# Four graph layers on one core: the 26 source tiles grouped as 4, 6, 6, 6, 4 instead of 6, 6, 6, 4, 4

## The chip, the cores and the metric

The kernel runs on one core of one Trainium2 chip. A core has five engines that work side by side, each through its own queue of instructions in order: TensorE (PE; its weight loads are listed apart as PEld), VectorE (DVE), ScalarE (ACT), GpSimd (POOL) and SyncE (SP), which here only issues transfers. They meet through semaphores. The metric is the device time of one execution in microseconds (us).

## What is computed

Four layers over a graph of 3327 nodes with 512 features and a dense 0/1 adjacency matrix. The first three are attention layers with 8, 4 and 8 heads, the last averages over neighbours. Each is applied to a normalised copy and added to the input:

```python
x = x + L0(relu(layernorm(x)), adj)     # 8 heads of 64
x = x + L1(relu(layernorm(x)), adj)     # 4 heads of 128, self loops added
x = x + L2(relu(layernorm(x)), adj)     # 8 heads of 64
x = x + L3(relu(layernorm(x)), adj)     # mean over neighbours, two dense layers

# an attention layer, for each head
e = leaky_relu(s1[:, None] + s2[None, :], 0.2)      # s1 = Wh @ a1, s2 = Wh @ a2
p = softmax(where(adj > 0, e, -inf), axis=1)
out = elu(p @ Wh)

# the last layer
agg = (adj > 0) @ x / max(degree, 1)
out = relu(concat(x @ W_self + b_self, agg @ W_nb + b_nb) @ W_comb + b_comb)
```

All of it is float32 in the reference.

## The kernel before

Layers are numbered `l` = 0 to 3 in the code; "the second layer" is `l == 1`.

**The two sides of leaky_relu.** exp(leaky_relu(s1 + s2)) is one product of a row factor and a column factor where s1 + s2 > 0, and another one where it is not. So a head needs two 0/1 matrices instead of real weights: the edges with a positive sum ("side" 0) and the edges with a negative sum (side 1). The column factors are multiplied into the projected features beforehand, the row factors after the sum.

**Tiles and groups.** The nodes are 26 tiles of 128. Target tiles are taken in seven chunks of four (the last has two). Source tiles `j` are taken in five groups, `JG` (L67): 6, 6, 6, 4 and 4 tiles. `JM` is the largest group and sizes the buffers. `jwhere` tells a tile's group and its place there. A group is the unit of a mask tile (`m`), of a load of features (`ab`), of the 0/1 tile (`tht`, `gt`), and of the copy to float32r.

**One head of one chunk** (`attention`, L603). SyncE loads the row scores `s1b` (L624) and the features `ab` (L634 in the second layer, one load per side and group; L601 in the others). For each source tile, ScalarE (L656) or VectorE (L653; the tiles of `GP_ON_DVE`, in the second layer 18 to 25) writes whether s1 + s2 > 0. VectorE ANDs a group with its mask (L662): side 0. An XOR with the mask gives side 1: L666 into `gt` in layers 1 and 3, and L722 in place in the second layer, after all reads of side 0. Then TensorE multiplies. A pass (L672) runs two target tiles over all 26 source tiles, with the 0/1 tile as weights and the features as moving data; sums stay in PSUM. VectorE adds the pieces up (L708 or L712), and L730 to L737 scale the head's result.

**Precision by group in the second layer** (`KIND`, L49, one letter a group). A "b" group keeps the features as three bf16 pieces side by side, 387 columns (L690), and uses the fp8 0/1 tile directly. In an "s" or "v" group the features are split into two float32r pieces, 258 columns (L687). Then the 0/1 tile must be float32r too: `real` (L585, its copy is L590) makes it once for each pass and group, on ScalarE into `ts` (3 buffers) for "s", on VectorE into `tv` (2 buffers) for "v". `KIND` is "bssvv". In layers 1 and 3 all features are bf16 pieces, with two matmuls for each pair of tiles (L694, L697).

**Preparing the next layer.** While a layer runs, finished target tiles go through normalisation, projection (L388) and splitting (`pieces`, L341, with L359 to L369, or L423 and L426 for float32r groups) for the next one. `hooks.run` (L718) does a step of that after each pass. A scheduler then lays out each engine's queue.

**The output stage** (L885 on). The third layer's last tiles are projected (L443), VectorE adds the bias (L450) and SyncE stores the rows (L453). `load_y2` (L770) brings the last layer's features, one load per group, on GpSimd's queue: group 0 during the last head, the others after it. Masks are copied to float32r (`mf`, six buffers), odd groups on VectorE (L916), even ones on ScalarE (L918). TensorE multiplies (L921); chunk 0 takes its four targets together, group by group, the others one at a time. L930 and L931 finish a row.

**Buffers.** All memory of a layer is laid out by hand in `tags` (L849 to L852), with a count of buffers for each name. A buffer is written again when its last reader is done. In the second layer `ab` has seven and `tht` ten.

Of the kernel before, what the change touches and what calls it, by code (L numbers as in the profile page):

```python
# [29 lines left out]
FP8 = mybir.dt.float8e4  # L30
F32R = mybir.dt.float32r
# [6 lines left out]
P = 128  # L38
# [14 lines left out]
def tile_gnn(ctx: ExitStack, tc: tile.TileContext, x, adj, W0, a01, W1, al, ar, W2, a2,  # L53
# [7 lines left out]
    def pn(t):  # L61
        return min(P, N - t * P)

    PER = 4
    chunks = [(t, min(PER, NT - t)) for t in range(0, NT, PER)]
    where = {t0 + k: (c, k) for c, (t0, n) in enumerate(chunks) for k in range(n)}
    JG = [(0, 6), (6, 6), (12, 6), (18, 4), (22, 4)]  # L67
    JM = max(n for _, n in JG)
    jwhere = {j0 + i: (g, i) for g, (j0, n) in enumerate(JG) for i in range(n)}
    heads = [8, 4, 8]  # L70
# [28 lines left out]
                for l in range(1, 4)]  # L99
    maskd = [[dram.tile([P, nt, nj, P], FP8, name=f"mask_{c}_{g}") for g, (_, nj) in enumerate(JG)]  # L100
             for c, (_, nt) in enumerate(chunks)]
# [11 lines left out]
    for l in range(3):  # L113
        H, DA, AO, HW = dims(l)
        if l == 1:
            abd.append([dram.tile([H, 2, P, nj, AO], BF16, name=f"ab{l}_{g}") if KIND[g] == "b" else
                        dram.tile([H, 2, P, nj, 2 * DA], F32, name=f"ab{l}_{g}") for g, (_, nj) in enumerate(JG)])
        else:
            abd.append([dram.tile([H, P, nj, HW], BF16, name=f"ab{l}_{g}") for g, (_, nj) in enumerate(JG)])
    y1d = [dram.tile([n * P, D], F32, name=f"y1_{c}") for c, (_, n) in enumerate(chunks)]  # L120
    y2d = [dram.tile([P, nj, 2, D], F32, name=f"y2_{g}") for g, (_, nj) in enumerate(JG)]
    Xd = [dram.tile([D, D], F32, name=f"X{i}") for i in range(2)]
# [480 lines left out]
    def attention(L, hooks, open_next, close):  # L603

        l = L.l
# [3 lines left out]
        for c, (t0, nt) in enumerate(chunks):  # L609
            W = nt * P  # L610
            last = c + 1 == len(chunks)
            A = [mp.tile([P, D], F32, name="A", bufs=A_BUFS[l]) for _ in range(nt)]
            hook = 0
            for h in range(H):
# [10 lines left out]
                ab = []  # L625
# [17 lines left out]
                th, flip = [[], []], []  # L643
                for g, (j0, nj) in enumerate(JG):

                    pt = mp.tile([P, PER * JM * P], FP8, name="tht", bufs=10 if l == 1 else 7)
                    gt = pt if l == 1 else mp.tile([P, PER * JM * P], FP8, name="gt", bufs=7)
                    gv = gt[:, :nt * nj * P].rearrange("p (k j i) -> p k j i", k=nt, j=nj)
                    pv = pt[:, :nt * nj * P].rearrange("p (k j i) -> p k j i", k=nt, j=nj)
                    for jj in range(nj):  # L650
                        j = j0 + jj
                        if j in GP_ON_DVE[l]:
                            nc.vector.tensor_scalar(gv[:, :, jj, :], s1v, L.ns2[:, j, h:h + 1], 2.0,  # L653
                                                    op0=ALU.is_gt, op1=ALU.mult, saturate=False)
                        else:
                            nc.scalar.activation(gv[:, :, jj, :], s1v, AF.Relu, bias=L.ks2[:, j, h:h + 1], scale=BIG,  # L656
                                                 saturate=False)
                    flat = "p k j i -> p (k j i)"
                    mu = masks[g].rearrange(flat).bitcast(U32)
                    gu = gt[:, :nt * nj * P].bitcast(U32)  # L660
                    pu = pt[:, :nt * nj * P].bitcast(U32)
                    nc.vector.tensor_tensor(pu, gu, mu, ALU.bitwise_and)  # L662
                    if l == 1:
                        flip.append((pu, mu))
                    else:
                        nc.vector.tensor_tensor(gu, pu, mu, ALU.bitwise_xor)  # L666
                    th[0].append(pv)
                    th[1].append(gv)
                R = mp.tile([P, PER, 2, DA], F32, name="R", bufs=1)
# [150 lines left out]
    with tc.tile_pool(name="first", bufs=1) as fp:  # L820
# [21 lines left out]
        while hooks.tiles or hooks.flying:  # L842
# [5 lines left out]
    A, R = [("A", D, F32, n) for n in A_BUFS], ("R", PER * 2 * 129, F32, 1)  # L848
    ab, gt, tht = ("ab", JM * 400, BF16, 7), ("gt", PER * JM * P, FP8, 7), ("tht", PER * JM * P, FP8, 7)  # L849
    tags = [[A[0], R, tht, ("gap", 15 * 1024, FP8, 1), gt],  # L850
            [A[1], ("ab", JM * 258, F32R, 7), R, ("ts", 2 * JM * P, F32R, 3), ("tv", 2 * 4 * P, F32R, 2), tht[:3] + (10,)],
            [A[2], ab, ("R", PER * 2 * 65, F32, 1), tht, gt]]  # L852
    hooks.masks = [lambda t=t, g=g: load_mask(ip, t, g) for t in range(NT) for g in range(len(JG))][hooks.done:]
    for l in range(3):
        att = ExitStack()
        if l == 2:
            yp = main.enter_context(tc.tile_pool(name="early", bufs=1, side="right", reuse_waits="tile"))
        mp = att.enter_context(tc.tile_pool(name=f"att{l}", bufs=1, reuse_waits="tile"))
        lay_out(mp, *tags[l])
        nxt = []  # L860

        def open_next():
            nxt.extend([open_layer(l + 1), Fusion(l, load_comb(l)) if l < 2 else None])
            return nxt[0]

        def close():
            return nxt[1]
        attention(L, hooks, open_next, close)
        att.close()
        if l == 0:  # L870
            masking.close()
        L = nxt[0]
# [512 lines left out]
```

## Time and profile before

| what | us |
|---|---|
| median of 3 runs (lowest to highest) | 3606.12 (3604.16 to 3607.49) |
| the profiled execution: its time | 3609.94 |
| the profiled execution: its span | 3608.1 |
| first layer's preparation, before its first attention matmul | 0 to 185 |
| first attention layer | 185 to 1278 |
| second attention layer (first to last matmul of L690 and L687) | 1278 to 2120 |
| third attention layer, with the turn of layers | 2120 to 3253 |
| turn to the output stage, and the output stage | 3253 to 3608 |

The stretches are from the first and last starts of the matmul lines. Within the second layer the matmuls of L687 and L690 are busy for 334.2 (on `ts`), 220.0 (on `tv`) and 226.1 us, L590's copies for 300.3 us on ScalarE and 145.9 on VectorE.

How to read the profile: the page shows one execution. A group line gives line, engine, operation, tiles (written <- read), shapes and count, then busy time in us and the mean ns of one; behind a second bar stand the engine's idle time just before such instructions and what ended it. A timeline line gives start and length in us, and behind the tiles how many instructions were merged into it. A line of waits says who waited for whom, with the us in total, the number of times and the longest. A row of stretches gives busy us and, in brackets, the number of instructions. Matmuls are pipelined, so that a line's mean is longer than the distance from one start to the next.

### The profile page before, as it was taken

The numbers are of one execution on the slowest core, as the hardware profiler recorded it, in microseconds if no ns is written. First come the engines' busy times: TensorE is split into PE (matmuls) and PEld (weight loads), VectorE is DVE, ScalarE is ACT, GpSimd is POOL, SyncE is SP. The second block draws the span as 40 slices with busy tenths as digits, with TensorE's granted clock in tenths as the row PEclk, the third lists the DMA queues.
The fourth block names the chain that finished last, engine by engine and source line by source line (L and its number), as shares of the span: only waits on it lengthen the run. The fifth ranks groups of instructions, "written<-read, shape, count | busy, mean of one in ns | idle before, by whom it ended". The sixth has DMA issues, their size and how long they took to land. (4 is left out here: it accounts for less than half of the span.)

```text
span 3608.1 us, 78551 instructions
## 1 busy us (share of the span) xinstructions
PE 3470.2 (96%) x31291; PEld 3131.4 (87%) x31291; DVE 2648.6 (73%) x5227; ACT 2511.8 (70%) x4113; POOL 603.0 (17%) x855
## 2 busy tenths in 40 slices
PE   6799999999999999999999989999999999999998
PEld 5589999999999878888888869989898989876886
DVE  7688888888887779888888868867676768672211
ACT  5587787777787788888788767767676767572111
POOL 6511221111110111233222230001010101010000
PEclk9899999999999999999999999999999999999999
DMA  7687777878866877877777876655555555576331
GB/s 213 213 239 219 212 217 215 229 207 234 237 194 206 297 264 272 286 254 277 278 257 271 311 265 205 194 176 181 175 191 182 169 176 189 169 270 253 101 104 52
DMA packets 369431, 780.69 MB, mean 216 GB/s; under 512 B 35906, under 2 KB 207333, under 8 KB 368416
## 3 DMA queue, kind: packets, MB, share of 16 engines
q1 hardware_dynamic: 341024, 713.17, 59.4%
q0 software_dynamic: 28032, 62.41, 7.3%
q8 instruction: 249, 4.08, 0.4%
q14 instruction: 126, 1.03, 0.1%
HBM read 667.96 MB, written 129.64 MB: 221 GB/s over the span
## 5 line engine op out<-in xcount | busy, mean ns | idle before, releaser
L694 PE MATMUL acc<-ab,tht 128*128 128x195 bf16 (+1 forms) x10816 | 1840.4, 248 | 15.6 <-DVE tht L662 14.3
L697 PE MATMUL acc<-ab,gt 128*128 128x195 bf16 (+1 forms) x10816 | 1839.4, 248 | 6.6 <-DVE rc L734 4.3
L656 ACT ACTIVATE gt<-s1b,ks 128x512 fp8e4<-128x512 f32 (+1 forms) x2464 | 1457.4, 677 | 316.5 <-issue 158.6
L694 PEld LDWEIGHTS <-tht 128*128 128x128 fp8e4 x10816 | 1059.1, 98 | 28.9 <-DVE tht L662 15.9
L697 PEld LDWEIGHTS <-gt 128*128 128x128 fp8e4 x10816 | 1058.9, 98 | 26.5 <-issue 20.2
L662 DVE TENSOR_TENSOR tht<-gt,m 128x768 uint32<-128x768 uint32 (+3 forms) x560 | 447.4, 799 | 141.4 <-ACT gt L656 139.5
L666 DVE TENSOR_TENSOR gt<-tht,m 128x768 uint32<-128x768 uint32 (+3 forms) x560 | 448.9, 802 | 8.7
L590 ACT CAST ts<-tht 128x1536 fp32r<-128x1536 fp8e4 x208 | 300.3, 1471 | 55.9 <-PE acc L687 51.7
L687 PE MATMUL acc<-ab,ts 128*128 128x258 f32 x2496 | 334.2, 290 | 4.4 <-ACT ts L590 2.3
L653 DVE TENSOR_SCALAR gt<-s1b,ns 128x512 fp8e4<-128x512 f32 (+1 forms) x448 | 222.2, 501 | 149.6 <-PE acc L697 147.9
L687 PEld LDWEIGHTS acc<-ab,ts 128*128 128x128 f32 x2496 | 314.1, 191 | 13.4 <-ACT ts L590 3.0
L921 PE MATMUL acc<-y,mf 128*128 128x512 f32 x1352 | 309.8, 391 | 1.6 <-DVE mf L916 1.6
L656 ACT ACTIVATE tht<-s1b,ks 128x512 fp8e4<-128x512 f32 (+1 forms) x504 | 308.5, 681 | 2.8 <-DMA s1b<-s 2.3
L921 PEld LDWEIGHTS acc<-y,mf 128*128 128x128 f32 x1352 | 253.5, 188 | 57.8 <-DVE mf L916 2.0
L712 DVE TENSOR_REDUCE R<-acc 128x130 f32<-128x390 f32 x416 | 214.5, 555 | 91.6 <-PE acc L697 91.0
L797 POOL TENSOR_TENSOR xt<-xt,e 128x512 f32<-128x512 f32 x72 | 122.2, 1697 | 888.8 <-DVE e L796 567.5
L690 PE MATMUL acc<-ab,tht 128*128 128x387 bf16 x1248 | 226.1, 329 | 6.0 <-DVE tht L662 3.2
L918 ACT CAST mf<-m 128x768 fp32r<-128x768 fp8e4 (+1 forms) x78 | 59.1, 762 | 245.1 <-PE acc L921 233.3
L687 PE MATMUL acc<-ab,tv 128*128 128x258 f32 x1664 | 220.0, 283 | 3.3 <-DMA ab<-ab 2.2
L687 PEld LDWEIGHTS acc<-ab,tv 128*128 128x128 f32 x1664 | 207.5, 189 | 6.2 <-issue 2.1
L388 PE MATMUL mm<-w,hT 128*128 128x260 f32 (+1 forms) x832 | 198.4, 393 | 9.3 <-ACT hT L141 5.6
L690 PEld LDWEIGHTS <-tht 128*128 128x128 fp8e4 x1248 | 117.3, 98 | 83.3 <-DVE tht L662 3.6
(141 smaller groups left out, 3421.4 us busy)
## 6 DMA issues: line engine op xcount, KB each, us to landing
ab<-ab SPq DMA_DIRECT2D x336, 600.0 KB, 5.6
ab<-ab SPq DMA_DIRECT2D x224, 400.0 KB, 4.1
ab<-ab SPq DMA_DIRECT2D x112, 774.0 KB, 6.3
ab<-ab SPq DMA_DIRECT2D x112, 516.0 KB, 5.5
ab<-ab SPq DMA_DIRECT2D x56, 582.0 KB, 6.6
s1b<-s SPq DMA_DIRECT2D x120, 256.0 KB, 6.2
m<-mask SPq DMA_DIRECT2D x72, 384.0 KB, 4.2
ab<-pt SPq DMA_DIRECT2D x13, 1600.0 KB, 7.6
```

Of the source, the lines that this page charges most:

```text
L388: L.mm = nc.tensor.matmul(pw, hT[:, k, :], L.w[:, k, f, :], start=(k == 0), stop=(k == KC - 1)).ins.name
L590: (nc.scalar.copy if KIND[g] == "s" else nc.vector.tensor_copy)(t[:, :k1 - k0, :nj], th[a][g][:, k0:k1])
L653: nc.vector.tensor_scalar(gv[:, :, jj, :], s1v, L.ns2[:, j, h:h + 1], 2.0, op0=ALU.is_gt, op1=ALU.mult, saturate=False)
L656: nc.scalar.activation(gv[:, :, jj, :], s1v, AF.Relu, bias=L.ks2[:, j, h:h + 1], scale=BIG, saturate=False)
L662: nc.vector.tensor_tensor(pu, gu, mu, ALU.bitwise_and)
L666: nc.vector.tensor_tensor(gu, pu, mu, ALU.bitwise_xor)
L687: mm = nc.tensor.matmul(acc[k][:, :2 * DA], thr[g][:, k - ks[0], jj, :], ab[a][g][:, jj, :], start=(j == 0), stop=(j == NT - 1), skip_grou ...
L690: mm = nc.tensor.matmul(acc[k][:, :3 * DA], th[a][g][:, k, jj, :], ab[a][g][:, jj, :3 * DA], start=(j == 0), stop=(j == NT - 1), skip_grou ...
L694: nc.tensor.matmul(acc[k][:, :3 * DA + o], th[0][g][:, k, jj, :], ab[0][g][:, jj, :3 * DA + o], start=(j == 0), stop=False, skip_group_che ...
L697: mm = nc.tensor.matmul(acc[k][:, AO:AO + 3 * DA + o], th[1][g][:, k, jj, :], ab[0][g][:, jj, AO:AO + 3 * DA + o], start=False, stop=(j == ...
L712: nc.vector.tensor_reduce(R[:, k], v.rearrange("p a (s d) -> p a d s", s=3), AX.X, ALU.add)
L921: nc.tensor.matmul(acc[k], mf[:, jj, :], y2[g][:, jj, s, :], start=(j0 + jj == 0 and s == 0), stop=(j0 + jj == NT - 1 and s == 1))
```

## The change

The groups become 4, 6, 6, 6, 4. `KIND` stays "bssvv": so in the second layer the "b" group has tiles 0 to 3 only, the two "s" groups 4 to 15 and the two "v" groups 16 to 25, ten tiles instead of eight. A `tv` buffer grows from four tiles to six, and `tht` has nine buffers instead of ten in that layer. All layers, the masks, the stored features and the output stage use the new groups; which tiles VectorE compares (`GP_ON_DVE`) stays.

```diff
-    JG = [(0, 6), (6, 6), (12, 6), (18, 4), (22, 4)]
+    JG = [(0, 4), (4, 6), (10, 6), (16, 6), (22, 4)]
...
-                    pt = mp.tile([P, PER * JM * P], FP8, name="tht", bufs=10 if l == 1 else 7)
+                    pt = mp.tile([P, PER * JM * P], FP8, name="tht", bufs=9 if l == 1 else 7)
...
-            [A[1], ("ab", JM * 258, F32R, 7), R, ("ts", 2 * JM * P, F32R, 3), ("tv", 2 * 4 * P, F32R, 2), tht[:3] + (10,)],
+            [A[1], ("ab", JM * 258, F32R, 7), R, ("ts", 2 * JM * P, F32R, 3), ("tv", 2 * JM * P, F32R, 2), tht[:3] + (9,)],
```

## The prediction

> **What bounds the kernel now.** I read the page first, then the stretches of the second layer, then the individual matmul starts there, then the waits, and last the few microseconds in which the third layer hands over to the output stage. The page says that TensorE is the bound over the whole span:
>
> ```profile
> PE 3470.2 (96%) x31291; PEld 3131.4 (87%) x31291; DVE 2648.6 (73%) x5227; ACT 2511.8 (70%) x4113; POOL 603.0 (17%) x855
> ```
>
> Only the second layer gets a different amount of work, so the stretches matter: chunk 0's heads 1 to 3 and a little more, the twenty heads of chunks 1 to 5, and the short last chunk. The columns are the stretch, its length, then the busy time of PE, PEld, DVE, ACT and POOL, the granted clock and the DMA load.
>
> ```profile
> 1299.00:1398.00 99.00, 97.46 (x748) 86.13 (x747) 92.46 (x180) 89.02 (x112) 1.31 (x2) 1.00 0.82 294
> 1398.00:2028.00 630.00, 626.72 (x4567) 550.19 (x4566) 550.17 (x1007) 538.13 (x724) 169.65 (x179) 1.00 0.76 268
> 2028.00:2120.00 92.00, 81.22 (x538) 69.02 (x537) 70.02 (x153) 59.06 (x102) 32.14 (x41) 0.94 0.92 342
> ```
>
> In chunks 1 to 5 TensorE is idle for 3.3 us of 630 and VectorE is busy 87%. In chunk 0 VectorE is at 93%, because nothing of the next layer is projected there and the heads are shorter. In the last chunk TensorE already waits 10.8 us.
>
> **The change part by part.** *(1) Matmuls.* 2 tiles x 26 target tiles x 4 heads x 2 sides = 416 matmuls change from bf16 with 387 columns (L690) to float32r with 258 (L687). Durations overlap, so I take starts: the first and the last L690 of one pass, then the second and the last L687 on ScalarE's copies.
>
> ```profile
> 1714.67 0.33 PE L690 MATMUL acc<-ab,tht 128*128 128x387 bf16 x1
> ...
> 1716.48 0.33 PE L690 MATMUL acc<-ab,tht 128*128 128x387 bf16 x1
> ...
> 1716.76 0.40 PE L687 MATMUL acc<-ab,ts 128*128 128x258 f32 x2
> ...
> 1719.42 0.28 PE L687 MATMUL acc<-ab,ts 128*128 128x258 f32 x1
> ```
>
> Eleven steps in 1.81 us are 0.1645 us each, twenty-two steps in 2.66 us are 0.121. The difference of 0.044 us times 416 is **-18.3 us** where TensorE is the bound: 0.70 us per full head of 31.5 us.
>
> The row of weight loads shows a median of 97 ns for L690 and 188 for L687, and still 24 of the latter fit into 3.01 us, so they overlap. [...] If a load of 188 ns set the step, these matmuls would cost 416 x (0.188 - 0.1645) = +9.8 us in place of a gain; the starts above show that it doesn't.
>
> *(2) VectorE's copies.* Of 208 casts of 1024 elements, 104 become casts of 1536. The trace has no such cast on VectorE; the nearest rows are these:
>
> ```profile
> L590 DVE CAST tv<-tht x208: 653/685/1545, 1292.1 to 2115.0; 128x1024 fp32r<-128x1024 fp8e4 x104
> L916 DVE CAST mf<-m 128x768 fp32r<-128x768 fp8e4 x26 | 14.3, 559 | 40.9 <-PE acc L921 40.9
> L916 DVE CAST mf<-m 128x512 fp32r<-128x512 fp8e4 x26 | 11.1, 427 | 117.0 <-PE acc L921 117.0
> ```
>
> 256 more elements cost 132 ns, and 1024 by that slope are 691 against the measured 685. So 1536 are 0.95 us and the edit adds 0.264 x 104 = 27.5 us to VectorE, 1.06 per full head. In chunks 1 to 5 VectorE goes from 27.5 to 28.6 us per head, where TensorE then needs 31.3 - 0.7 = 30.6: 93%, hidden behind L687 and L690. In chunk 0, where a head is four passes of 6.79 us (first L690 to first L690), 27.2 in all, VectorE's 92.46 becomes 92.46 + 3.6 x 1.06 = 96.3, and TensorE's 97.46 - 3.6 x 0.7 = 94.9: there VectorE becomes the bound. I give the 4 heads' 2.8 us back and add 0.5: **+3.3** (ends: 0, and 2.8 + 4 x 1.06 = 7.0 if no idle time of VectorE takes any of it). In the last chunk ScalarE and transfers hold TensorE up, so I give back its two head equivalents: **+1.4** (ends 0 and 2.5).
>
> *(3) Waits in the second layer.* A copy of group 3 now frees its `tv` buffer after 12 matmuls instead of 8, and one buffer of `tht` goes. With nine, group 4 of the next head reuses group 0 of this head, so VectorE's four L653 for tiles 22 to 25 wait for the last pass's eight L690. Behind them on VectorE stand L662, the next `tv` casts and L708; TensorE waits for them at tile 22, about 11 us later, so it is covered by most of two passes of 6.6 us. If that cover went, each of 24 heads could lose about 2.6 us of L653 and L662. Transfers of `ab` grow by 2 tiles x 128 x 256 bytes x 2 sides x 28 heads = 3.7 MB. A float32r group can be issued when the buffer seven loads earlier is read for the last time, and is needed one pass and one group later, 6.79 + 12 x 0.121 = 8.2 us (now 8.1), against a median landing of 6.0 us; group 3 goes from 516 to 774 KB and joins the larger ones. TensorE's waits now:
>
> ```profile
> PE acc L687 <- DMA ab<-ab: 2.3, 5, 1.2
> PE acc L687 <- DVE tv L590: 0.6, 2, 0.4
> ```
>
> The bounds for all this together are -2.9 us (both rows vanish) and +13.7 (3.7 MB at the 268 GB/s of that stretch, all exposed). I take **+3.0**, nearer the rows, which show that such waits are rare.
>
> *(4) The output stage.* It has the same tiles and matmuls, but chunk 0 runs group by group over four targets, and the first group shrinks from 48 matmuls to 32.
>
> ```profile
> 3278.15 15.23 SPq L453 DMA_DIRECT2D y<-AB  x2
> 3280.26 11.77 PE L921 MATMUL acc<-y,mf 128*128 128x512 f32 x48
> ...
> 3292.43 0.69 DVE L450 TENSOR_TENSOR AB<-mm,bias 128x512 f32<-128x512 f32 x1 [14.30 <-DMA y<-AB]
> 3293.03 1.96 DVE L916 CAST mf<-m 128x768 fp32r<-128x768 fp8e4 x4
> ...
> 3293.64 6.64 PE L921 MATMUL acc<-y,mf 128*128 128x512 f32 x28 [1.60 <-DVE mf L916]
> ```
>
> The casts of group 1 stand on VectorE behind an L450 that waits 14.3 us for a store, which lands when the loads of `y2` have landed. The built program keeps that order. The first group's matmuls cover this wait; of them 16 x 0.2286 us (298.08 us for 1304 in the chain of waits) = 3.7 us go behind it. The load of group 3 grows by 1 MB, 2.4 us at the 425 GB/s seen from 3275 to 3285, and delays the store. The stall of about 8 us can also lower the clock: after idle time at 3262 to 3269 it was 0.83 and 0.66, worth 1.7 us at most. Ends 3.7 and 7.8; I take 3.7 + 2.4 + 0.6 = **+6.7**.
>
> *(5) Nothing else.* Tiles 4 and 5 are prepared in layer 1 by L423 and L426 (4 x about 0.65 us) in place of L359, L363, L367 and L369 (1.23 + 4 x 0.63 + 2 x 1.17): less on ScalarE and GpSimd, 0.15 more per tile on VectorE, all behind L694 and L697. Heads of layers 1 and 3 have the same instructions and bytes in another order; buffers are still read 32 tiles before their next need. At a layer's start TensorE follows ScalarE's L656 (0.6 us a tile against 0.33): the first matmul comes about 1 us earlier, and the sixth tile of group 3 makes the end of the first pass up to 1 us later, within +-1 for each of three starts, taken as 0.
>
> Sum: -18.3 + 3.3 + 1.4 + 3.0 + 6.7 = -3.9. The profiled execution took 3609.94 us, its span 3608.1 and 1.8 around it, 3.8 above the median of the runs; 3609.94 - 3.9 = 3606.0, and on the median's scale 3606.12 - 3.9 = **3602.2**.
>
> **The rivals.** *A, VectorE has room.* Chunk 0 already shows VectorE at 93% with TensorE at 98%, so casts might fit everywhere and the new waits stay out: -18.3 + 1.4 + 6.7 = -10.2, **3595.9** (3591 with the last chunk's gain and the milder output stage). Against it: VectorE's queue is in order, and chunk 0 has no slack by the sum above. *B, VectorE's queue becomes the bound of the second layer (slower).* In chunks 1 to 5 its 80 us of idle time are 47.3 us of waits of L590 for L687 and 13.4 of L722 for L590's copies, which an in-order queue keeps if they are not slack. If it keeps all, each full head grows by 1.06 us instead of shrinking: +27.5 + 6.7 = +34; if half of the casts' added time is absorbed, 13.8 + 6.7 = +20, **3626**. It decides from the point where less than 1.3 us of the 4.0 us of idle time per head can be given up (1.06 - 1.3 = -0.26, times 26 heads, is the output stage's 6.7). For it: the shorter window for L653. Against: 87% now. *C, the output stage covers itself.* If the store lands before the first group is through, (4) falls away: -18.3 + 7.7 = -10.6, **3595.5**. Against it: it landed last of everything in the trace.
>
> **How the numbers follow.** The forecast, a small net gain, gets 0.50, its own range 3594 to 3610; A 0.15, C 0.08, B 0.27 (from 3610 up). A measurement of this kernel can tell about 0.2%, 7.2 us. Of the forecast's half I put 0.13 below 3598.9 and 0.37 between the bounds; A and C are faster; of B 0.25 lies above 3613.3. So faster 0.36, same 0.39, slower 0.25. The range leaves 0.08 below and 0.12 above: from A's better side 3591 to the milder part of B, 3621.
>
> **What would show it.** Right: TensorE's span of the second layer 8 to 14 us shorter with starts of 0.1645 and 0.121 kept; casts of 1536 at 0.95 us; VectorE at 92 to 94% in chunks 1 to 5 and almost full in chunk 0, no shorter than now; the first L921 group of 32 followed by 6 to 8 us without a matmul, ended by L916. Wrong: waits of L690 or L687 for L662 or L590 adding up to over 10 us in chunks 1 to 5 (B), or a seamless start of the output stage (C).

## The result, and the profile after

The changed kernel takes 3621.59 us (median of 6 runs, 3618.92 to 3626.21), the kernel before 3605.77 (6 runs beside them, 3604.16 to 3608.86). The ratio is 1.004, with a 95% interval of 1.003 to 1.005: slower by 16 us, where 4 us faster was forecast. The profiled execution of the changed kernel took 3626.21 us with a span of 3624.4, which is 16.3 more than the span before. Its page opens with:

```profile
PE 3457.3 (95%) x31291; PEld 3144.8 (87%) x31291; DVE 2675.3 (74%) x5229; ACT 2500.5 (69%) x4109; POOL 598.9 (17%) x849
```

TensorE has 12.9 us less work than before (3470.2), as meant, and yet ends 16 us later: it waits about 29 us more. To see where, I took the starts of the first and last matmul of each stage from the two traces, in us:

| stage (from start to start) | before | after | difference |
|---|---|---|---|
| first layer: first L694 to first L690 | 1092.9 | 1096.1 | +3.2 |
| second layer, chunk 0 | 124.0 | 120.3 | -3.7 |
| second layer, chunks 1 to 5 | 630.0 | 626.8 | -3.2 |
| second layer, last chunk to the last L687 | 87.5 | 95.8 | +8.3 |
| third layer: first to last L694 | 1109.5 | 1116.8 | +7.3 |
| output stage: last L694 to last L921 | 338.2 | 345.0 | +6.8 |

The start-up and the turn between the second and the third layer are 1.2 and 1.3 shorter. The stretches of the second layer that the prediction began with (length; then busy time of PE, PEld, DVE, ACT, POOL; granted clock; DMA share and GB/s) now read as follows, the later two cut at the first L690 of chunk 1 and of the last chunk:

```profile
1299.00:1398.00 99.00, 98.12 (x769) 90.04 (x767) 94.66 (x178) 84.84 (x103) 1.58 (x4) 1.00 0.88 307
1400.30:2027.10 626.80, 614.96 (x4566) 558.04 (x4564) 577.30 (x1010) 538.75 (x733) 173.46 (x179) 1.00 0.78 275
2027.10:2122.90 95.80, 76.71 (x500) 66.47 (x499) 69.50 (x148) 57.88 (x103) 34.98 (x41) 0.91 0.88 321
```

In chunks 1 to 5 VectorE is at 92% and TensorE idle for 11.8 us instead of 3.3; in the last chunk for 19 instead of 10.8. An undisturbed pass did become shorter, from 6.79 to 6.60 us between its L690 groups. So the gain is there pass by pass, and something between the passes takes it back. The waits of 1400 to 2030 us show what:

```profile
DVE tv L590 <- PE acc L687: 27.4, 18, 3.5
...
DVE AB L407 <- ACT AB L401: 8.7, 5, 2.9
...
PE acc L687 <- DVE tv L590: 7.1, 9, 1.3
...
PE acc L687 <- DMA ab<-ab: 4.0, 7, 1.6
```

TensorE's wait for VectorE's copies was 0.6 us in the whole kernel before. The wait of L407 is new: five times, once in each chunk, VectorE waits for the exponentials that ScalarE makes for the next layer's tile (L401). VectorE's queue at one of the five places, at the turn to the last head of a chunk:

```profile
1742.24 1.02 DVE L708 TENSOR_REDUCE R<-acc 128x129 f32<-128x387 f32 x2
1746.12 1.29 DVE L407 TENSOR_TENSOR AB<-mm,AB 128x512 f32<-128x512 f32 x2 [2.86 <-ACT AB L401]
1747.32 1.22 DVE L730 TENSOR_TENSOR R<-R,cpm 128x1032 f32<-128x1032 f32 x1
1748.46 0.68 DVE L590 CAST tv<-tht 128x1024 fp32r<-128x1024 fp8e4 x1
...
1752.70 2.51 DVE L737 TENSOR_SCALAR A<-R,rc 128x128 f32<-128x128 f32 x4
1755.13 0.94 DVE L590 CAST tv<-tht 128x1536 fp32r<-128x1536 fp8e4 x1
```

and TensorE at the same time:

```profile
1749.20 1.23 PE L687 MATMUL acc<-ab,tv 128*128 128x258 f32 x8 [1.29 <-DVE tv L590]
...
1756.13 2.76 PE L687 MATMUL acc<-ab,tv 128*128 128x258 f32 x20 [1.06 <-DVE tv L590]
```

L407 stands ahead of the copy in VectorE's order and idles for 2.86 us, with the copy behind it; the copy ends when TensorE has been out of work for 1.29 us. The next copy stands behind L359 and L737 and is 1.06 us late. The pair costs 2.4 us and comes back at the same place of other chunks, 126.8 us earlier and 126.4 later (1.6 and 1.9 us). Before, L407 stood in the same pass and waited for nothing, but what stood around it was in another order:

```profile
1746.93 0.96 DVE L722 TENSOR_TENSOR tht<-tht,m 128x768 uint32<-128x768 uint32 x1 [1.17 <-ACT ts L590]
1747.80 1.02 DVE L708 TENSOR_REDUCE R<-acc 128x129 f32<-128x387 f32 x2
1748.74 1.28 DVE L407 TENSOR_TENSOR AB<-mm,AB 128x512 f32<-128x512 f32 x2
...
1751.08 0.69 DVE L590 CAST tv<-tht 128x1024 fp32r<-128x1024 fp8e4 x1
...
1753.22 0.69 DVE L590 CAST tv<-tht 128x1024 fp32r<-128x1024 fp8e4 x1
...
1755.04 2.51 DVE L737 TENSOR_SCALAR A<-R,rc 128x128 f32<-128x128 f32 x4
```

An L722 stood ahead of L407, and VectorE did its waiting before that; the next pass's copy stood ahead of L737. In the changed kernel the scheduler puts both behind. ScalarE's L401 also comes later in the pass: 3.8 us after its first L690 (1745.88 after 1742.11), where it was 1.6 (1747.42 after 1745.82). So the change touched the order of the queues too, and not only the length of the copies. Why ScalarE is later there, no run isolates.

In the last chunk one wait stands out. ScalarE's queue there, and TensorE's matmul that waits for its last line:

```profile
2052.01 2.89 ACT L656 ACTIVATE tht<-s1b,ks 128x256 fp8e4<-128x256 f32 x7
2054.81 1.45 ACT L590 CAST ts<-tht 128x1536 fp32r<-128x1536 fp8e4 x1
2056.17 2.50 ACT L656 ACTIVATE tht<-s1b,ks 128x256 fp8e4<-128x256 f32 x6
2058.57 1.45 ACT L590 CAST ts<-tht 128x1536 fp32r<-128x1536 fp8e4 x1
2059.93 0.57 ACT L141 COPY hT<-tp 128x512 f32<-128x512 f32 x1
```
```profile
2060.56 1.69 PE L388 MATMUL mm<-w,hT 128*128 128x264 f32 x3 [6.91 <-ACT hT L141]
```

Thirteen masks and two copies of the next head stand ahead of the 0.57 us that TensorE needs. The wait was 1.0 us before. Later in that chunk an L687 waits 4.6 us for ScalarE's copy, where it was 2.3; in e6 and e9 below it is 4.6 as well.

In the third layer TensorE now stops three times for 0.5 to 0.8 us at each of five changes of chunk, 9.7 us in all, where it stopped once, 3.4 us in all; here one change, first as it is now, then as it was:

```profile
2498.29 0.24 PE L697 MATMUL acc<-ab,gt 128*128 128x195 bf16 x1 [0.61 <-DVE gt L666]
2501.01 0.26 PE L694 MATMUL acc<-ab,tht 128*128 128x195 bf16 x1 [0.62 <-DVE tht L662]
2502.04 0.24 PE L697 MATMUL acc<-ab,gt 128*128 128x195 bf16 x1 [0.77 <-DVE rc L734]
```
```profile
2495.75 0.24 PE L697 MATMUL acc<-ab,gt 128*128 128x195 bf16 x1 [0.66 <-DVE rc L734]
```

And the output stage begins like this (the SPq line merges the issues of two stores, the second right behind the L450 below):

```profile
3286.01 19.30 SPq L453 DMA_DIRECT2D y<-AB  x2
3288.12 8.02 PE L921 MATMUL acc<-y,mf 128*128 128x512 f32 x32
...
3304.35 0.69 DVE L450 TENSOR_TENSOR AB<-mm,bias 128x512 f32<-128x512 f32 x1 [18.37 <-DMA y<-AB]
3304.96 1.48 DVE L916 CAST mf<-m 128x768 fp32r<-128x768 fp8e4 x3
...
3305.57 0.79 PE L921 MATMUL acc<-y,mf 128*128 128x512 f32 x1 [9.42 <-DVE mf L916]
```

The first group of 32 matmuls is through at 3296.1; L450 holds the casts of the next group until the first store has landed, some 18 us after its issue, and TensorE stands for 9.4 us.

### The profile page after: what moved, and what is told of

It reads as the page before. It is cut to its first block, busy times and chain, and to the rows that moved or that the text cites. A ratio compares the mean times of both kernels' runs of the same rounds, so it can differ in the third digit from the quotient of the medians.

```text
span 3624.4 us, 78609 instructions
## 1 busy us (share of the span) xinstructions
PE 3457.3 (95%) x31291; PEld 3144.8 (87%) x31291; DVE 2675.3 (74%) x5229; ACT 2500.5 (69%) x4109; POOL 598.9 (17%) x849
## 5 line engine op out<-in xcount | busy, mean ns | idle before, releaser
L694 PE MATMUL acc<-ab,tht 128*128 128x195 bf16 (+1 forms) x10816 | 1845.9, 248 | 14.8 <-DVE tht L662 13.7
L694 PEld LDWEIGHTS <-tht 128*128 128x128 fp8e4 x10816 | 1060.9, 98 | 28.6 <-DVE tht L662 15.7
L687 PE MATMUL acc<-ab,ts 128*128 128x258 f32 x2496 | 334.4, 290 | 7.6 <-ACT ts L590 4.6
L687 PEld LDWEIGHTS acc<-ab,ts 128*128 128x128 f32 x2496 | 313.9, 191 | 16.5 <-ACT ts L590 6.0
L590 ACT CAST ts<-tht 128x1536 fp32r<-128x1536 fp8e4 x208 | 299.7, 1468 | 32.9 <-PE acc L687 16.3
L921 PE MATMUL acc<-y,mf 128*128 128x512 f32 x1352 | 310.5, 392 | 9.4 <-DVE mf L916 9.4
L921 PEld LDWEIGHTS acc<-y,mf 128*128 128x128 f32 x1352 | 254.6, 188 | 65.2 <-DVE mf L916 9.9
L653 DVE TENSOR_SCALAR gt<-s1b,ns 128x512 fp8e4<-128x512 f32 (+1 forms) x448 | 211.0, 476 | 109.4 <-PE acc L697 108.8
L687 PE MATMUL acc<-ab,tv 128*128 128x258 f32 x2080 | 271.2, 284 | 11.1 <-DVE tv L590 7.7
L687 PEld LDWEIGHTS acc<-ab,tv 128*128 128x128 f32 x2080 | 257.3, 189 | 16.4 <-DVE tv L590 11.9
L918 ACT CAST mf<-m 128x512 fp32r<-128x512 fp8e4 (+1 forms) x78 | 53.5, 690 | 259.1 <-PE acc L921 249.2
L388 PE MATMUL mm<-w,hT 128*128 128x260 f32 (+1 forms) x832 | 200.3, 395 | 15.3 <-ACT hT L141 12.9
L590 DVE CAST tv<-tht 128x1536 fp32r<-128x1536 fp8e4 x208 | 179.1, 863 | 35.6 <-PE acc L687 35.5
L388 PEld LDWEIGHTS mm<-w,hT 128*128 128x128 f32 x832 | 158.7, 196 | 42.6 <-ACT hT L141 17.3
```

The source lines that it names most:

```text
L388: L.mm = nc.tensor.matmul(pw, hT[:, k, :], L.w[:, k, f, :], start=(k == 0), stop=(k == KC - 1)).ins.name
L590: (nc.scalar.copy if KIND[g] == "s" else nc.vector.tensor_copy)(t[:, :k1 - k0, :nj], th[a][g][:, k0:k1])
L687: mm = nc.tensor.matmul(acc[k][:, :2 * DA], thr[g][:, k - ks[0], jj, :], ab[a][g][:, jj, :], start=(j == 0), stop=(j == NT - 1), skip_grou ...
L694: nc.tensor.matmul(acc[k][:, :3 * DA + o], th[0][g][:, k, jj, :], ab[0][g][:, jj, :3 * DA + o], start=(j == 0), stop=False, skip_group_che ...
L921: nc.tensor.matmul(acc[k], mf[:, jj, :], y2[g][:, jj, s, :], start=(j0 + jj == 0 and s == 0), stop=(j0 + jj == NT - 1 and s == 1))
```

## The experiments

Ratios are to the kernel before, run on the same chip between them, with 95% intervals; the changed kernel stands at 1.004. The stages are from one profiled execution each, in us, as in the table above.

| run | ratio | layer 1 | layer 2 | layer 3 | output |
|---|---|---|---|---|---|
| before | 1 | 1092.9 | 841.4 | 1109.5 | 338.2 |
| after | 1.004 (1.003 to 1.005) | 1096.1 | 842.9 | 1116.8 | 345.0 |
| e1_before_tht9 | 1.0027 (1.0015 to 1.0038) | 1095.0 | 853.1 | 1109.9 | 339.9 |
| e2_after_tht10 | 1.0033 (1.002 to 1.0046) | 1096.6 | 846.4 | 1116.7 | 345.1 |
| e3_after_dve6 | 1.0032 (1.0022 to 1.0042) | 1097.4 | 839.6 | 1115.1 | 344.9 |
| e4_after_y | 0.9999 (0.9989 to 1.0009) | 1092.1 | 842.8 | 1117.0 | 334.0 |
| e5_after_cast4 | 1.0019 (1.001 to 1.0029) | 1092.4 | 836.1 | 1116.8 | 346.7 |
| e6_after_shift | 0.999 (0.9981 to 1.0) | 1099.0 | 829.0 | 1117.2 | 345.2 |
| e7_after_sizes | 1.0104 (1.0087 to 1.0121) | 1097.3 | 865.3 | 1116.9 | 346.8 |
| e8_after_l3_8 | 1.0001 (0.9991 to 1.0011) | 1093.4 | 842.6 | 1106.1 | 344.4 |
| e9_after_all | 0.993 (0.9916 to 0.9944) | 1089.3 | 826.1 | 1106.3 | 334.0 |
| e10_before_all | 0.9999 (0.999 to 1.0007) | 1095.0 | 846.1 | 1108.2 | 336.1 |
| e11_all_layer1 | 0.9909 (0.9893 to 0.9925) | 1087.2 | 826.9 | 1106.0 | 334.0 |
| e12_all_tht10 | 0.9933 (0.9919 to 0.9948) | 1094.6 | 830.5 | 1106.9 | 334.0 |

The table has its own measure of chance. The second layer is the same code in the changed kernel, e4 and e8: 842.9, 842.8, 842.6. The third layer is untouched in the changed kernel and e2 to e7: 1116.7 to 1117.2 in six of these seven, 1115.1 in e3. But the first layer is untouched in everything from the changed kernel to e8 and lies between 1092 and 1099. The output stage is untouched in the changed kernel and all of e2 to e8 but e4, and lies between 344.4 and 346.8. So the +3.2 of the first layer is no finding, and the other stages can be read to 1 or 2 us.

### The missing buffer: e1 and e2

e1, on the kernel before:

```diff
-                    pt = mp.tile([P, PER * JM * P], FP8, name="tht", bufs=10 if l == 1 else 7)
+                    pt = mp.tile([P, PER * JM * P], FP8, name="tht", bufs=9 if l == 1 else 7)
...
```

> The kernel before with nine buffers of tht in the second layer instead of ten, and nothing else. Theory 1 (VectorE's added casts make the copies of group 3 late): the second layer stays within 2 us of the kernel before, 3606 us. Theory 2 (the missing buffer makes the masks of the next head late): in chunks 1 to 5 waits of L687 and L690 grow by 6 to 10 us, the last chunk shows a wait of several us for L656's late tiles as the changed kernel does (6.9), and the time is 3614 to 3622.

The second layer grows by 11.7 us: 4.8 in chunks 1 to 5 and 6.8 in the last chunk. There the wait of the changed kernel appears, with the groups and the copies of before (waits between 2027 and 2132 us):

```profile
PE mm L388 <- ACT hT L141: 5.4, 1, 5.4
```

So in the old grouping the tenth buffer is worth 11.7 us, as theory 2 says, though less of it lies in chunks 1 to 5 than expected. e2 gives it back to the changed kernel:

```diff
-        t = mp.tile([P, 2, nj, P], F32R, name="ts" if KIND[g] == "s" else "tv", bufs=3 if KIND[g] == "s" else 2)
+        t = mp.tile([P, 2, nj, P], F32R, name="ts" if KIND[g] == "s" else f"tv{g}", bufs=3 if KIND[g] == "s" else 1)
...
-                    pt = mp.tile([P, PER * JM * P], FP8, name="tht", bufs=9 if l == 1 else 7)
+                    pt = mp.tile([P, PER * JM * P], FP8, name="tht", bufs=10 if l == 1 else 7)
...
```

> The changed kernel with the tenth buffer of tht back; room for it comes from giving group 3 and group 4 a buffer of their own size in place of two of six tiles (each group still has one). Theory 1: chunks 1 to 5 stay at about 627 us, and VectorE's busy time there at 577; the time stays within 3 us of 3621.6, or loses only the last chunk's wait of 6.9. Theory 2: chunks 1 to 5 fall to 616 to 620 us, the last chunk's wait of 6.9 for hT goes, and the time is 3603 to 3610.

Neither came out clean: the last chunk gains 3.2 us (92.6) and its wait of 6.9 falls only to 4.7, but chunks 1 to 5 take 630.8, with waits for loads of `ab` of 8.1 instead of 4.0, and the layer is 3.5 longer. The buffer that cost 11.7 us in the one grouping brings nothing in the other. Theory 2 falls as the explanation of chunks 1 to 5; of the last chunk's 8.3 us it may hold some 3.

### VectorE's load or its queue: e3, e5, e6

e3 relieves VectorE of two comparisons a head, e5 of the added part of the copies (its lines after 589 stand one further down):

```diff
-GP_ON_DVE = [(5, 12, 19), tuple(range(18, 26)), (4, 9, 14, 19, 24)]
+GP_ON_DVE = [(5, 12, 19), tuple(range(20, 26)), (4, 9, 14, 19, 24)]
```
```diff
-        (nc.scalar.copy if KIND[g] == "s" else nc.vector.tensor_copy)(t[:, :k1 - k0, :nj], th[a][g][:, k0:k1])
+        m = 4 if KIND[g] == "v" else nj
+        (nc.scalar.copy if KIND[g] == "s" else nc.vector.tensor_copy)(t[:, :k1 - k0, :m], th[a][g][:, k0:k1, :m])
...
-                                    mm = nc.tensor.matmul(acc[k][:, :2 * DA], thr[g][:, k - ks[0], jj, :], ab[a][g][:, jj, :],
+                                    mm = nc.tensor.matmul(acc[k][:, :2 * DA], thr[g][:, k - ks[0], jj % 4 if KIND[g] == "v" else jj, :], ab[a][g][:, jj, :],
```

> The changed kernel with the comparisons (L653) of tiles 18 and 19 in the second layer given to ScalarE (L656): VectorE is relieved of 2 x 0.47 = 0.94 us a head, close to what the casts added (1.06), and ScalarE gets 2 x 0.62 = 1.24 more on 27 of 31 us. Theory 1: the waits of L687 for L590 (7.7 us) halve at least and chunks 1 to 5 fall from 627 to 619 to 623 us; the time is 3613 to 3618. Theory 2: no gain, and a loss of 0 to 5 us, since ScalarE's L656 come even later: 3621 to 3627.

> The changed kernel in which VectorE's copy of group 3 takes four of the six tiles; the matmuls of the other two read the copies of the first two again, so that all matmuls, loads and buffers stay and the output is not the reference's. VectorE loses exactly what the change added, 104 x 0.264 = 27 us. Theory 1 (VectorE's added time): TensorE's waits of L687 for L590 in chunks 1 to 5 (7.1 us) fall below 2.5, these chunks take 616 to 620 us in place of 627, chunk 0 118 in place of 120, and the whole is 9 to 14 us shorter than the changed kernel. Theory 3 (the place of the copies in VectorE's queue behind the next layer's tile, L407 waiting for ScalarE's L401, decides, not their length): the waits fall by less than half and chunks 1 to 5 take 623 to 627 us.

In e3 VectorE has 12.3 us less work in chunks 1 to 5 (565.0 after 577.3) and TensorE waits for its copies as long as before (7.2 us, nine times), as L407 does for L401 (8.1 us, now ten times); the stretch gains 3.8 us. Its 623.0 us are the upper end of what theory 1 gave, but not by the waits that theory 1 named. That speaks against the mere amount without excluding it. In e5 the wait is gone (1400 to 2030 us):

```profile
PE acc L688 <- DVE tv L591: 0.5, 2, 0.3
```

and still chunks 1 to 5 take 623.3 us, 3.5 less, where theory 1 wanted 616 to 620; the last chunk gains 4.1. The run doesn't part the two theories, since with the shorter copies the order changes as well: at the turn shown above, VectorE's queue is again that of the kernel before (the XOR ahead of L407, the next copy ahead of the scaling of A), and L407 waits for nothing in these chunks. Other waits remain, 4.6 us of them for loads of `ab`, and the stretch stays 7 us above the 615.9 that the matmuls alone would give (630.0 - 320 x 0.044).

e6 leaves all the work and moves the next layer's tiles by one pass, in the second layer only:

```diff
-                        hooks.run(1 if last else 3, hook, 2 if hook % 2 and c == 0 or hook % 3 == 0 and c else 1, 2 if last else 1)
+                        hooks.run(1 if last else 3, hook + 2 if l == 1 else hook, 2 if hook % 2 and c == 0 or hook % 3 == 0 and c else 1, 2 if last else 1)
```

> The changed kernel with the stages of the next layer's tiles in the second layer begun after passes 1, 4, 7 and 10 of a chunk instead of 0, 3, 6 and 9, so that L401 and L407 of the third tile no longer fall on the turn to the last head, where L730 to L737 stand too. Theory 3: the pair of waits there (1.29 and 1.06 us in one chunk, 10 us in all five) goes, chunks 1 to 5 take 617 to 621 us in place of 627, the time is 6 to 10 us shorter than the changed kernel. Rival: VectorE is 92% busy, so the same waits turn up at another pass, and chunks 1 to 5 stay within 3 us of 627.

Chunks 1 to 5 take 618.0 us, 8.8 less, the last chunk 89.1, 6.7 less, and the kernel is 0.005 faster than the changed one. VectorE still has the whole load (574.5 us busy of these 618.0). Its queue at the corresponding turn to the last head, where L407 now comes after L737 and waits for nothing:

```profile
1744.74 0.86 DVE L737 TENSOR_SCALAR A<-R,rc 128x128 f32<-128x128 f32 x4
...
1749.46 0.95 DVE L590 CAST tv<-tht 128x1536 fp32r<-128x1536 fp8e4 x1
...
1751.30 1.29 DVE L407 TENSOR_TENSOR AB<-mm,AB 128x512 f32<-128x512 f32 x2
1752.51 0.69 DVE L590 CAST tv<-tht 128x1024 fp32r<-128x1024 fp8e4 x1
```

The waits between 1400 and 2030 us are, in this kernel:

```profile
PE acc L687 <- DMA ab<-ab: 4.4, 5, 1.7
...
PE acc L687 <- DVE tv L590: 1.3, 2, 0.7
```

L407 waits for L401 for 0.9 us in all these chunks, where it was 8.7. So in chunks 1 to 5 it was the place in the queues and not the amount of work. The edit moves all steps of a tile, so it doesn't show that L407 alone made the difference. That the last chunk gains too was not foreseen: the wait of L388 for L141 fell there from 6.9 to 0.4 us. The tile started one pass later meets other work of ScalarE; the experiment doesn't show more of it than that.

### More buffers by size: e7

```diff
-                        tl = mp.tile([P, JM * 2 * DA], F32R, name="ab", bufs=7)
+                        tl = mp.tile([P, nj * 2 * DA], F32R, name=f"ab{nj}", bufs=4 if nj == 6 else 4)
...
-                    pt = mp.tile([P, PER * JM * P], FP8, name="tht", bufs=9 if l == 1 else 7)
+                    pt = mp.tile([P, PER * (nj if l == 1 else JM) * P], FP8, name=f"tht{nj}" if l == 1 else "tht",
+                                 bufs=(6 if nj == 6 else 4) if l == 1 else 7)
...
-        t = mp.tile([P, 2, nj, P], F32R, name="ts" if KIND[g] == "s" else "tv", bufs=3 if KIND[g] == "s" else 2)
+        t = mp.tile([P, 2, nj, P], F32R, name="ts" if KIND[g] == "s" else f"tv{g}", bufs=3 if KIND[g] == "s" else 2 if g == 3 else 1)
...
```

> The changed kernel with buffers of the second layer kept by size, so that the groups of four tiles no longer take six-tile buffers: six and four of tht (every group of two heads has one), two for the copies of group 3 and one for group 4, four large and four small of ab in place of seven large. Theory 2 (buffers): a copy of group 3 can then be made a whole pass ahead and the masks a whole head ahead; waits of L687 for L590 fall below 3 us, the last chunk's wait of 6.9 for hT goes, and the second layer takes 828 to 834 us in place of 843. If the order of the queues alone decides, it stays within 4 us of 843. With only four large buffers of ab, waits for the loads of ab could also grow from 4 to 8 us or more, which would show as such.

A miss: the second layer takes 865.3 us. The copies are in time (1.2 us of waits), and the wait that the last sentence names is far larger than said (1400 to 2030 us):

```profile
PE acc L688 <- DMA ab<-ab: 24.0, 26, 4.0
```

Four large buffers of `ab` are too few for three large groups a side. With TensorE held up there, the run says nothing about theory 2, and the copies may be in time for that reason alone.

### The output stage: e4

```diff
-                y = pre.tile([P, D], F32, name="AB", bufs=1)
+                y = pre.tile([P, D], F32, name="hT" if behind else "AB", bufs=2 if behind else 1)
```

> The changed kernel with the four late sums of L450 written into the two buffers of hT, free by then, instead of the one of AB, so that no L450 waits for the store of another. Theory (step 4 of the prediction: L450's wait for the store holds up the casts L916 behind it): the wait of L450 (18.4 us) goes, TensorE's wait of 9.4 for L916 falls to under 2, the stage from the last L694 to the last L921 falls from 345 to 336 to 338 us and the time to 3613 to 3615. Rival (the loads of y2 are late themselves): TensorE waits as long at the same place, now for the load of y2, and the time stays at 3621.6 within 2.

The wait is gone and with it the gap; VectorE and TensorE of this kernel, at the same place:

```profile
3282.89 0.69 DVE L450 TENSOR_TENSOR hT<-mm,bias 128x512 f32<-128x512 f32 x1 [2.74 <-PE mm L443]
3283.50 1.02 DVE L916 CAST mf<-m 128x768 fp32r<-128x768 fp8e4 x2
```
```profile
3282.29 20.09 PE L921 MATMUL acc<-y,mf 128*128 128x512 f32 x85
```

85 matmuls run on without a gap of note. The stage falls by 11.0 us to 334.0, which is 4.2 below the kernel before: the shorter stall that was there already (1.6 us for L916, behind 14.3 of L450) is gone too, and the granted clock, 0.83 in 3263 to 3273 of the kernel before, is 1.00 from 3256 to 3310 here. The rival falls: the loads of `y2` were there. The gain is 1.6 more than the wait of 9.4, and the granted clock, 0.70 in the 4 us behind that wait in the changed kernel, tells of it (last section).

### The third layer: e8

```diff
-                    pt = mp.tile([P, PER * JM * P], FP8, name="tht", bufs=9 if l == 1 else 7)
-                    gt = pt if l == 1 else mp.tile([P, PER * JM * P], FP8, name="gt", bufs=7)
+                    pt = mp.tile([P, PER * JM * P], FP8, name="tht", bufs=9 if l == 1 else 8 if l == 2 else 7)
+                    gt = pt if l == 1 else mp.tile([P, PER * JM * P], FP8, name="gt", bufs=8 if l == 2 else 7)
...
```

> The changed kernel with eight buffers of tht and of gt in the third layer instead of seven (the first group of y2 has become smaller, which leaves room). Theory 4 (at a change of chunk only the first two groups of the next head stand ready, ten tiles now where it was twelve, and ScalarE makes the next ones only after the sums of the finished chunk): the two waits of 0.8 us at each of the five changes go, the third layer's attention takes 1109 to 1111 us in place of 1117, the time is 5 to 8 us shorter than the changed kernel. Rival: ScalarE's queue, where L794 and L795 wait for GpSimd's L797, holds the masks up whatever the buffers are: 1115 to 1117 us as now.

The third layer takes 1106.1 us: 10.7 less, and 3.4 less than before the change. ScalarE's queue at a change of chunk shows how. First the changed kernel:

```profile
2480.38 0.63 ACT L794 ACTIVATE e<-A 128x512 f32<-128x512 f32 x1 [0.28 <-DVE A L737]
...
2485.26 0.63 ACT L794 ACTIVATE e<-A 128x512 f32<-128x512 f32 x1 [3.59 <-POOL xt L797]
...
2488.74 0.63 ACT L794 ACTIVATE e<-A 128x512 f32<-128x512 f32 x1 [2.18 <-POOL xt L797]
...
2489.94 12.96 ACT L656 ACTIVATE gt<-s1b,ks 128x512 fp8e4<-128x512 f32 x21
```

then e8:

```profile
2477.14 0.63 ACT L794 ACTIVATE e<-A 128x512 f32<-128x512 f32 x1 [2.10 <-POOL xt L797]
...
2478.34 12.96 ACT L656 ACTIVATE gt<-s1b,ks 128x512 fp8e4<-128x512 f32 x21
2491.21 0.62 ACT L794 ACTIVATE e<-A 128x512 f32<-128x512 f32 x1
```

In the changed kernel the sums of the finished chunk stand in ScalarE's queue one behind the other, each waiting for GpSimd, and the 21 masks of the next head come after three of them, 9.6 us after the first. The kernel before had the same three sums there, for 8.5 us (2476.37 to 2484.84); so what differs is how much is ready when they begin, by the count of buffers two groups of the next head in both, ten tiles in place of twelve. With an eighth buffer a head's masks can be written earlier, the order puts them between the sums, and the waits at the change are no longer in the list. Theory 4 and its rival named the two halves of one thing: ScalarE's queue holds the masks up, and the buffer lets them go ahead.

### Everything together: e9 to e12

e9 is the changed kernel with the edits of e4, e6 and e8; e10 the kernel before with those of e4 and e6. e11 adds to e9 eight buffers in the first layer, and e12 the tenth buffer of `tht`, with the copies' buffers of e2. The diff after the four expectations is e11's, against e9. (A diff above that ends in `...` leaves out the matching counts in `tags`.)

> The changed kernel with the three edits that each took away one loss when made alone: the late sums of L450 in buffers of their own, the next layer's tiles begun one pass later in the second layer, eight buffers of tht and gt in the third layer. If the three losses are separate, the gains add: 11 + 14 + 11 = 36 us less than the changed kernel, 0.986 to 0.990 of the kernel before. If they share one cause or hand the wait on, less than 25 us less: above 0.993.

> The kernel before with the two of these edits that it has room for (L450's buffers, the tiles one pass later; the eighth buffers of the third layer don't fit beside its larger first group of y2). It has no long wait in its second layer and only 1.6 us for L916, so if the repairs mend what the regrouping broke, it gains 2 to 6 us: 0.998 to 1.0. If the edits are good in themselves, whatever the groups, it gains 15 us or more: below 0.996, and the second layer takes less than 835 us.

> The changed kernel with the three edits, and eight buffers of tht and gt in the first layer too (6 KB taken from the gap between them). If the change of chunk costs there what it did in the third layer, the first layer falls from 1092 to 1099 us by 5 to 10 and the time is 0.002 below the kernel with the three edits; if its limit is elsewhere (its heads also make masks and project), no difference over 2 us.

> The changed kernel with the three edits and ten buffers of tht in the second layer, made room for by copies' buffers of their own size. If the missing buffer costs in the new grouping too, as its absence cost the kernel before 11.7 us, the second layer falls from 829 us by 4 to 10; if with the smaller first group nine are enough, it stays within 3.

```diff
-                    pt = mp.tile([P, PER * JM * P], FP8, name="tht", bufs=9 if l == 1 else 8 if l == 2 else 7)
+                    pt = mp.tile([P, PER * JM * P], FP8, name="tht", bufs=9 if l == 1 else 8)
...
-    tags = [[A[0], R, tht, ("gap", 15 * 1024, FP8, 1), gt],
+    tags = [[A[0], R, tht[:3] + (8,), ("gap", 9 * 1024, FP8, 1), gt[:3] + (8,)],
```

e9 is at 0.993, some 0.011 or 40 us under the changed kernel: the three gains add up. (The 36 us of the expectation, taken from 1.004, would have been 0.994; its figures in ratios had been taken from the kernel before by mistake.) Its chunks 1 to 5 take 616.5 us, 13.5 less than before the change, and its TensorE is idle for 138 us of the span of 3578.4, after 167 in the changed kernel and 138 before.

e10 is at 0.9999. The output stage gains 2.1 us, the second layer loses 4.7: begun one pass later, the tiles are better placed in the new grouping and worse in the old. So the later tiles are not good in themselves; they mend what the regrouping broke. The buffers of L450 help in both groupings, and the eighth buffers had no room in the old one, so their worth there is open. Of what e9 gains on the kernel before, the second layer's 15.3 us belong to the regrouping with its tiles moved; the third layer's 3.2 and the output stage's 4.2 may be the edits' own in part.

e11 is the fastest kernel measured here, 0.9909, but its interval overlaps that of e9 and the first layer's 1087.2 us lies within what that layer varies by, so the worth of its own edit stays open. e12 settles the tenth buffer: 830.5 us against 826.1, no gain.

## Why the prediction was wrong, step by step

*(1) Matmuls, -18.3: right.* In chunks 1 to 5 passes are 0.19 us shorter for the four matmuls that changed in each, against 4 x 0.044 = 0.18, and with the waits mended (e9) 13.5 of the 14.1 us arrive. The weight loads of L687, 191 ns on average on `ts` and 189 on `tv` in the changed kernel, do not set the step: from the first of 24 such matmuls of a pass to the first on `tv` it is 3.02 us (1719.19 to 1722.21), 0.126 a matmul.

*(2) Copies, +27.5 us of VectorE: right in the duration* (0.94 to 0.96 us against 0.95), *too dear in its consequences.* Chunk 0 was to come out 0.5 longer, with VectorE as its bound; it came out 2.5 to 3.7 shorter in the three runs of the same code (124.0 against 120.3, 121.2 and 121.5), with VectorE busy for 94.66 of 99 us. VectorE's idle time did absorb most of it.

*(3) Waits in the second layer, +3.0: this is the step that failed first.* The layer was to be 10.6 us shorter (-18.3 + 3.3 + 1.4 + 3.0) and was 1.5 longer: with (1) and (2) as written, the term should have been 15.1, beyond its upper bound of 13.7. As chunk 0 didn't need its 3.3, the waits cost more still: 10.9 in chunks 1 to 5 (626.8 - 615.9) and 9.7 in the last chunk (8.3, and the 1.4 that its matmuls gained). I had bounded the term by loads of `ab` and by buffers, asked what stands behind L653, and taken the order of the queues as given. The cost came from an instruction that the change doesn't touch: L407, which waits for ScalarE, with copies behind it that are needed in the same pass, in an order that had changed with the copies; and in the last chunk L141 behind ScalarE's masks. e6 takes 13.9 us away by moving the steps of the tiles to which both belong.

*(4) Output stage, +6.7: right in place and cause* (the store holds L450, L450 holds L916), *and in size partly by luck* (+6.8). The stall is 9.4 us after 1.6, longer than the 6 to 8 that I gave as a sign, and the clock, 0.70 in the next 4 us, takes about 1 us behind it, where I had put 0.6; against that, the kernel before ran at a clock of 0.83 in the 10 us from 3263, and the changed one at 1.00 from 3262 to 3282. e4 shows that the whole stall can be had back, and what was already there before.

*(5) Nothing else: wrong for the third layer, +7.3.* I had argued that buffers are read 32 tiles before their next need, which holds inside a chunk. At a change of chunk ScalarE's queue is blocked by the sums for about 9 us, and what counts is how many tiles stand ready: 4 + 6 now, 6 + 6 before. That cost 1.5 us at each of five changes; e8 shows that one more group ready takes it away.

Of the rivals, B forecast nearly the right time, 3626, by luck: VectorE's queue was to become the bound since it keeps its waits, and 13.8 of B's 20 us were to come in the second layer, which grew by 1.5; the third layer's 7.3 it didn't have. The queue gave up waits (of L590 for L687, 27.4 us after 47.3), B's sign of over 10 us of waits for the copies and masks stayed away (7.3), and e6 and e9 carry the same work without the loss. Its turning point of 1.3 us should read 1.32 (1.06 + 0.26). A, VectorE has room, is what e9 shows in chunks 1 to 5. C fell; the first group didn't cover the store.

## What to carry to other kernels

An engine at 87% has room for more work only where its queue has it: look for the instruction ahead of the lengthened one that waits for another engine (here L407, 8.7 us in chunks 1 to 5), and add that wait to the sum. Where a scheduler lays out the queues, a changed length can change the order too: compare the order before and after. When groups change their size, count how many tiles stand ready at each place where an engine's queue is blocked (a change of chunk, the turn to another stage), since a share of busy time shows none of these. And when a change gains in every undisturbed pass and loses as a whole, look for the repeating stalls between the passes and mend those: here three small edits turned +0.4% into -0.7%.

## What the runs showed of the hardware

The long stall of the output stage cost more than its length. The rows of stretches at the start of the changed kernel's output stage (busy PE, PEld, DVE, ACT, POOL; granted clock; DMA) read:

```profile
3296.00:3306.00 10.00, 0.58 (x2) 0.43 (x2) 1.65 (x4) 0.83 (x1) 0.00 (x0) 0.61 0.57 239
3306.00:3310.00 4.00, 4.00 (x14) 3.11 (x14) 0.92 (x2) 0.05 (x1) 0.00 (x0) 0.70 0.06 17
3310.00:3316.00 6.00, 6.00 (x28) 4.99 (x27) 0.56 (x1) 1.61 (x2) 0.00 (x0) 1.00 0.85 292
```

After 9.4 us without work the granted clock is 0.70 for four more microseconds in which TensorE is busy throughout, 14 matmuls in place of some 18 (28 in 6 us in the last row); that is about 1 us of the 1.6 that e4 gained beyond the wait. By single microseconds the granted clock is 1.00 up to 3298, 0.59 in the next, 0.50 in each from 3299 to 3308, 0.79 in the next and 1.00 from 3309 on. So it went down about 2 us after the last matmul ahead of the stall (which ended at 3296.1) and was back about 3 us after the first one behind it (3305.57). A stop of 2.09 us in the kernel before (3260.3 to 3262.4) has 0.50 from 3265 to 3268 behind it; one of 2.09 us in the changed kernel (3269.8 to 3271.9) has 1.00. How long a stop must be, these rows don't show.

What had not been expected is how little the second layer's time depends on VectorE's amount of work (12.3 us less of it in chunks 1 to 5 of e3 gained 3.8 us) and how much on the order: nine or ten buffers, or one pass earlier or later, move the second layer by 12 to 14 us in one grouping, and in the other by 3 to 5 the other way.
